# A planned four-layer graph kernel: when a PSUM bank is opened, seven-block left products in a third gated step, and ten units in the chip

## The chip, the cores and the metric

The kernel runs on one core of a Trainium2 chip. The core has a matrix engine (TensorE, written PE in the profile, with its weight loads as PEld), a vector engine (VectorE, DVE), an activation engine (ScalarE, ACT), a general engine (GpSimd, POOL) and a queue that only issues transfers (SyncE, SP). Each engine runs its own instructions in the order in which the program lists them. The metric is the device time of one execution in microseconds (us), the median of several runs. PSUM is the memory that TensorE writes its products into; the kernel treats it as eight banks of 128 partitions by 512 float32 values.

## What is computed

The input `x` is 64 graphs of 256 nodes with 128 features, all in float32, and `adj` is one 256 by 256 matrix of zeros and ones that all graphs share. Four layers follow one another, each of the form "add the layer's result to its input and normalize each node":

```
x = layernorm(x + attention_0(x, adj))            # softmax attention, plus x @ self_weight
x = layernorm(x + attention_1(x, adj))            # softmax attention, elu
x = layernorm(x + gated(x, adj))                  # five gated steps
x = layernorm(x + chebyshev(x, adj))              # products with adj, adj^2, adj^3 folded

# one gated step, of five:
m = adj @ h                                       # the "left product", per graph
z = sigmoid((m, m) @ w3.T + h @ u3.T)
r = sigmoid((m, m) @ w4.T + h @ u3.T)
v = tanh((m, m) @ w5.T + (r * h) @ u5.T)
h = (1 - z) * h + z * v
```

The gated layer is where most of the matrix work lies and where the change acts.

## The kernel before

**Tiling.** A unit is two graphs, so there are 32 units. Everything that a unit needs lies in a lane, a set of fixed tiles; `LANES = 9` lanes exist, unit `u` uses lane `u % 9`, and a lane is given to its next unit when the unit in it has issued its last instruction. So up to nine units are in the chip at once.

**The planner.** No loop sets the order of the instructions. The functions `layer0` to `layer3` only record tasks with `add(engine, ns, fn, reads, writes, after)`, where `ns` is what the planner takes the task to cost on its engine. `Plan.run` then plays the engines forward: whenever an engine is free it takes, among its tasks whose inputs are ready and for which enough PSUM banks are free, the one with the least key (`first`, line 963). The key is the unit's number times `PERIOD` plus the task's due time within its unit; due times grow along a unit's chain and are stretched by `PACE` (`PACE_GATED` in the gated layer). The last units, one for each lane, get keys that lie close together, counted back by `LATE` and `TAIL`. The instructions are emitted in the order that this gives, and each engine later executes its own in exactly that order, with waits where data is not there yet.

**PSUM banks.** A bank is taken by the first task that writes to it and is given back once every task that uses it has ended. A product whose inputs are early may therefore open a bank long before the other products that go into the same bank can run.

**The gated layer (`layer2`, line 823).** Per step and unit there is first the left product. The plain form is `left` (line 767): two graphs times two halves of the nodes, four matmuls of 128x128 by 128x256 at line 771 into one bank, and a copy of the bank to `m` by ScalarE (line 839). The fast form is `left_fast` (line 775): the two halves of the nodes and the two by two blocks of `adj` are combined so that seven matmuls of 128x128 by 128x128 (line 788) do what eight such blocks do, with three VectorE sums before them (lines 781 to 784), a ScalarE copy of one block (line 800), and four VectorE sums after them (lines 815 to 821), in two banks. Which steps use it is set by `FAST = (3, 4)`, and also asks that the step's input came by way of memory (`far`, below).

Five products by 128x512 follow, all at line 843 through the helper `product`. In the text they go by their weights: gT3, with the old state h, opens the bank `ps_g`; gT1, with m, completes the sum for r; ScalarE takes tanh of it (line 852) and VectorE forms r times h (line 854). gT2, with m, opens the bank `ps_v`; gT0, with m, is added into `ps_g` and turns the sum for r into the sum for z (line 859 takes its tanh); u5T, with r times h, completes `ps_v` (line 868 takes its tanh). VectorE then forms the new state (lines 866, 870, 872).

**Turning the state.** The next left product needs the state with nodes on the partitions. Where `far(u, step)` holds, VectorE transposes 32 by 32 blocks (lines 880, 893, 525) and transfers through a memory buffer move the blocks (`hb`, then `ht`, lines 883 to 901). Where it does not hold, TensorE does it by four transposes (line 905, and line 512 at the layer's ends), which is quicker for one unit but uses TensorE. `FIRST_FAR` makes the first two units use TensorE early on, `LAST_FAR = {0: -1, 1: 1}` makes the last unit (31) use it throughout and unit 30 from its step 1 on.

**Loading.** The first `XDIRECT = 9` units load x in its natural layout, by one transfer, and transpose it on TensorE (line 512). Later units load it by four transfers with the blocks already exchanged, and VectorE transposes the blocks (line 606).

Of the kernel before, what the change touches and what calls it, by code (L numbers as in the profile page):

```python
# [13 lines left out]
P = 128  # L14
NEG = -1.0e30
EPS = 1e-5
STEPS = 5
LANES = 9
LEAD = 10
BANKS = 8  # L20
BL = 32
FAST = (3, 4)
NORM = (0, 1, 2, 3)
SCALES = True
TIGHT = 4
FIRST_FAR = {0: 2, 1: 2}
LAST_FAR = {0: -1, 1: 1}
PERIOD = 43e3
TAIL = 0.3
LATE = 5  # L30
PACE = 2.6
PACE_GATED = 1.56
HOLD = 80
DIRECT_ROWS = 3
XDIRECT = 9
START = 35e3
R2 = 1
R3 = 1.5
# [158 lines left out]
def kernel(  # L197
# [28 lines left out]
    nc = tc.nc  # L226
# [6 lines left out]
    PE, DVE, ACT, POOL = "pe", "dve", "act", "pool"  # L233
# [12 lines left out]
    plan = Plan([psum.tile([P, 512], F32, tag=f"ps{k}", name=f"ps{k}") for k in range(BANKS)])  # L246
    add = plan.add
# [4 lines left out]
    def mm_ns(cols, n=1):  # L252
        return n * (cols * 1.667 + 5)
# [163 lines left out]
    for t, wT, n in ((wx0, woT, C0), (ws0, wselfT, D + 2)):  # L417
        ps = bank()
# [22 lines left out]
    gT = transposed("gT", [(gs[0], gs[0].ap), (gs[1], gs[1].ap), (gs[2], gs[2].ap), (u3, u3.ap)])  # L441
# [43 lines left out]
    for mc in range(NC):  # L485
        for kc in range(NC):
            add(PE, mm_ns(N), lambda mc=mc, kc=kc: nc.tensor.matmul(
                ps_a2.ap[:, mc * N : (mc + 1) * N], adj_t.ap[:, kc, mc * P : (mc + 1) * P], adjT.ap[:, kc, :],
                start=(kc == 0), stop=(kc == NC - 1)), (adj_t, adjT), (ps_a2,))
# [69 lines left out]
    def layernorm(u, L, pairs, swap=False, centred=False):  # L559

        st, ve, rstd = L["st"], L["ve"], L["rstd"]
        sts, xs = object(), object()
        for k, (c, view) in enumerate(pairs):
            add(DVE, 330, lambda k=k, view=view: nc.vector.bn_stats(st.ap[:, k, :], view().rearrange("p j d -> p d j")),  # L566
                (c,), (st,), group=sts)
        add(DVE, 150, lambda: nc.vector.tensor_scalar(  # L568
            ve.ap.rearrange("p (k j) -> p k j", k=2), st.ap.rearrange("p k (j s) -> p k j s", j=2)[:, :, :, 2], 1.0 / D, EPS,
            op0=ALU.mult, op1=ALU.add), (st,), (ve,))  # L570
        add(POOL, 1050, lambda: nc.gpsimd.tensor_tensor(rstd.ap, ve.ap, nhalf.ap, op=ALU.pow), (ve, nhalf), (rstd,))  # L571
        by_act = u >= TIGHT and plan.layer in NORM

        if by_act and not centred:
            add(DVE, 120, lambda: nc.vector.scalar_tensor_tensor(
                ve.ap.rearrange("p (k j) -> p k j", k=2), st.ap.rearrange("p k (j s) -> p k j s", j=2)[:, :, :, 1], -1.0,
                rstd.ap.rearrange("p (k j) -> p k j", k=2), op0=ALU.mult, op1=ALU.mult), (st, rstd), (ve,))
        for k, (c, view) in enumerate(pairs):
            for j in range(2):
                b, ch = (j, k) if swap else (k, j)  # L580
                at = slice(2 * k + j, 2 * k + j + 1)
                shift, col = (ones, slice(0, 1)) if centred else (ve, at)
                if by_act:
                    add(ACT, 300, lambda j=j, b=b, ch=ch, view=view, at=at, shift=shift, col=col: nc.scalar.activation(  # L584
                        X[u].ap[:, b, ch, :], view()[:, j, :], AF.Identity, bias=shift.ap[:, col], scale=rstd.ap[:, at]),
                        (c, shift, rstd), (X[u],), group=xs)
                elif centred:
                    add(DVE, 260, lambda j=j, b=b, ch=ch, view=view, at=at: nc.vector.tensor_scalar(
                        X[u].ap[:, b, ch, :], view()[:, j, :], rstd.ap[:, at], 1.0, op0=ALU.mult, op1=ALU.add),
                        (c, rstd), (X[u],), group=xs)  # L590
                else:
                    add(DVE, 260, lambda k=k, j=j, b=b, ch=ch, view=view, at=at: nc.vector.tensor_scalar(
                        X[u].ap[:, b, ch, :], view()[:, j, :], st.ap[:, k, 3 * j + 1 : 3 * j + 2], rstd.ap[:, at],
                        op0=ALU.subtract, op1=ALU.mult), (c, st, rstd), (X[u],), group=xs)
# [6 lines left out]
    def layer0(u, L):  # L601
# [7 lines left out]
        lc, d, e, p, h, u4, cu = L["m"], L["d"], L["e"], L["p"], L["h0"], L["u"], L["cu"]  # L609
        nm, s, rs = L["nm"], L["s"], L["rs"]  # L610
        hs, es, ss, ps_, ds_ = object(), object(), object(), object(), object()
        for b in range(UB):
# [5 lines left out]
            for c in range(NC):  # L618
                add(PE, mm_ns(C0), lambda b=b, c=c, hv=hv: nc.tensor.matmul(  # L619
                    hv()[:, c, :], xb[:, b, c * P : (c + 1) * P], wx0.ap, start=(c == 0), stop=True,  # L620
                    skip_group_check=True), (xT, wx0), (hx,))
# [18 lines left out]
        else:  # L640
            ds = bank()
            for b in range(UB):
                for k in range(2):
                    add(PE, 240, lambda b=b, k=k: nc.tensor.matmul(
                        ds.ap[:, b : b + 1], xb[:, b, k : N : 2], wx0.ap[:, D + 2 + k : D + 3 + k],
                        start=(k == 0), stop=(k == 1)), (xT, wx0), (ds,))
# [5 lines left out]
                neg0.ap[:, :, 0:P].rearrange("p k (c i) -> p k c i", c=NC)), (row, neg0), (e,), group=es)  # L652
        for b in range(UB):
            if SCALES and u >= TIGHT:
                add(ACT, 370, lambda b=b: nc.scalar.activation(
                    ev[:, b, :, P:N], neg0.ap[:, :, P:N], AF.Identity, bias=d.ap[:, b : b + 1]), (d, neg0), (e,), group=es)
            else:
                add(DVE, 260, lambda b=b: nc.vector.tensor_scalar_add(ev[:, b, :, P:N], neg0.ap[:, :, P:N], d.ap[:, b : b + 1]),
                    (d, neg0), (e,), group=es)
# [11 lines left out]
        tail = [add(DVE, 120, lambda: nc.vector.reciprocal(rs.ap, s.ap), (s,), (rs,))]  # L671
        hq = object()
        for g in range(G if SCALES and u >= TIGHT else 0):
            add(ACT, 270, lambda g=g: nc.scalar.activation(
                h.ap[:, g, 0 : D + 2], h.ap[:, g, 0 : D + 2], AF.Copy, scale=rs.ap[:, g : g + 1]), (h, rs), (h,), group=hq)
        if not SCALES or u < TIGHT:
            add(DVE, 700, lambda: nc.vector.tensor_mul(
# [4 lines left out]
        for b in range(UB):  # L682
            y = bank()
# [5 lines left out]
            for c in range(NC):  # L689
                add(PE, mm_ns(D + 2), lambda b=b, c=c, yv=yv: nc.tensor.matmul(  # L690
                    yv()[:, c, :], xb[:, b, c * P : (c + 1) * P], ws0.ap, start=(c == 0), stop=False,
                    skip_group_check=True), (xT, ws0), (y,), tail)
# [82 lines left out]
    def left_fast(src, blk, mat, s, p1, m):  # L775


        four = gd(s.ap)
        ss = object()

        add(DVE, 360, lambda: nc.vector.tensor_sub(
            four[:, 0:2], blk(slice(2, 3)).to_broadcast([P, 2, D]), blk(slice(0, 4, 3))), (src,), (s,), group=ss)
        add(DVE, 220, lambda: nc.vector.tensor_sub(four[:, 2:3], four[:, 1:2], blk(slice(0, 1))), (src, s), (s,), group=ss)
        add(DVE, 220, lambda: nc.vector.tensor_add(four[:, 3:4], four[:, 2:3], blk(slice(1, 2))), (src, s), (s,), group=ss)
        x, y = bank(), bank()

        def one(ps, at, lhs, k, c, cells):
            add(PE, mm_ns(P), lambda: nc.tensor.matmul(  # L788
                ps.ap[:, at * P : (at + 1) * P], lhs(), mat.ap[:, k, c * P : (c + 1) * P], start=True, stop=True,
                skip_group_check=True), (*cells, mat), (ps,), group=four)  # L790

        def a(g):
            return lambda: blk(slice(g, g + 1))[:, 0]

        def sm(k):
            return lambda: four[:, k]


        one(x, 0, a(0), 0, 0, (src,))
        add(ACT, 280, lambda: nc.scalar.copy(p1.ap[:, 0:P], x.ap[:, 0:P]), (x,), (p1,))  # L800
        one(x, 1, a(1), 1, 0, (src,))
        one(y, 3, a(3), 3, 1, (src,))
        one(y, 1, sm(0), 3, 0, (s,))
        one(y, 0, sm(1), 2, 0, (s,))
        one(x, 2, sm(2), 2, 1, (s,))
        one(y, 2, sm(3), 1, 1, (s,))
        mv = gd(m.ap)

        ms = object()

        def pv(ps):
            return gd(ps.ap)


        add(DVE, 400, lambda: nc.vector.tensor_tensor(
            mv[:, 0:4:3], pv(x)[:, 1:3], p1.ap[:, 0:P].rearrange("p (o n) -> p o n", o=1).to_broadcast([P, 2, P]), op=ALU.add),
            (x, p1), (m,))
        add(DVE, 400, lambda: nc.vector.tensor_tensor(
            mv[:, 1:3], pv(y)[:, 0:2], mv[:, 3:4].to_broadcast([P, 2, P]), op=ALU.add), (y, m), (m,))
        add(DVE, 240, lambda: nc.vector.tensor_add(mv[:, 3:4], pv(y)[:, 0:1], mv[:, 2:3]), (y, m), (m,))  # L820
        add(DVE, 400, lambda: nc.vector.tensor_add(mv[:, 1:3], pv(y)[:, 2:4], mv[:, 1:3]), (y, m), (m,))

    def layer2(u, L):
        h, ht = turned(u, L, -1), X[u]
        for step in range(STEPS):
            m = L["m"]
            fast = step in FAST and far(u, step - 1)
            ps_m = None if fast else bank()
            if fast:
# [9 lines left out]
                add(ACT, 500, lambda ps_m=ps_m: nc.scalar.copy(m.ap, ps_m.ap), (ps_m,), (m,))  # L839
            ps_g, ps_v = bank(), bank()  # L840

            def product(ps, w, c, rhs, start, stop):
                add(PE, mm_ns(T), lambda: nc.tensor.matmul(ps.ap, w(), rhs.ap, start=start, stop=stop,  # L843
                                                           skip_group_check=True), (c, rhs), (ps,))

            product(ps_g, lambda: gT.ap[:, 3], gT, h, True, False)
            product(ps_g, lambda: gT.ap[:, 1], gT, m, False, True)
            r, z, v = L["r"], L["z"], L["v"]

# [1 line left out]
            up = part if step else 1.0  # L851
            add(ACT, 600, lambda ps_g=ps_g, up=up: nc.scalar.activation(  # L852
                r.ap, ps_g.ap, AF.Tanh, bias=bias2.ap[:, 1:2], scale=0.5 / up), (ps_g, bias2), (r,))
            add(DVE, 600, lambda h=h: nc.vector.scalar_tensor_tensor(r.ap, r.ap, 1.0, h.ap, op0=ALU.add, op1=ALU.mult),  # L854
                (r, h), (r,))
            product(ps_v, lambda: gT.ap[:, 2], gT, m, True, False)
            product(ps_g, lambda: gT.ap[:, 0], gT, m, False, True)
            product(ps_v, lambda: u5T.ap[:, 0], u5T, r, False, True)
            add(ACT, 600, lambda ps_g=ps_g, up=up: nc.scalar.activation(  # L859
# [14 lines left out]
            h = new  # L874
# [128 lines left out]
```

## Time and profile before

| | before |
|---|---|
| median of 3 runs | 1424.1 us (1423.8 to 1427.39) |
| span of the profiled execution | 1422.9 us |
| TensorE busy | 1408.2 us, 99% of the span, 6009 matmul records |
| VectorE busy | 1082.7 us, 76% |
| ScalarE busy | 954.1 us, 67% |
| GpSimd busy | 141.5 us, 10% |
| transfers | 143.27 MB, 101 GB/s on average |

A float32 matmul of the program stands in the trace as two matmul records, each with a weight load of its own; a transpose is one record. Records of matmuls that run one after another overlap, [...] so the mean duration in a group (594 ns for 128x512) is longer than the distance from one start to the next. The distance is what counts for the sum of the work. It can be read off the chain that ended last, which lists unbroken runs of one kind with their length and number.

In the groups by line, the part after the bar is the busy time, the mean of one, and the idle time just before these instructions with what ended it. Idle time of VectorE and ScalarE costs nothing in itself while TensorE has other work.

### The profile page before, as it was taken

The page shows a single profiled execution, that of the slowest core. Times are in us where ns is not written, and L with a number is a line of the kernel's source. Part 1 is how long each engine was busy: PE and PEld are TensorE (multiplying, and loading weights), DVE is VectorE, ACT ScalarE, POOL GpSimd, SP SyncE. Part 2 cuts the span into 40 slices and gives each one's busy share as a digit, 9 for nine tenths or more (in the row PEclk, how much of TensorE's full clock was granted, in tenths as well). Part 3 has the DMA queues.
Part 4 walks back from the last instruction along what each step waited for, and adds up shares of the span by engine and source line. Part 5 has one row for each costly group of instructions (what it writes and reads, how often), then busy time and mean ns, then how long its engine had stood idle before and what let it go on. Part 6 is the DMA issues. An engine that isn't in the chain of part 4 may idle for free.

```text
span 1422.9 us, 19902 instructions
## 1 busy us (share of the span) xinstructions
PE 1408.2 (99%) x6009; PEld 959.7 (67%) x6009; DVE 1082.7 (76%) x2521; ACT 954.1 (67%) x2132; POOL 141.5 (10%) x134
## 2 busy tenths in 40 slices
PE   9999999999999999999999999999999999999998
PEld 8766666666766666766666666767666665666676
DVE  7977877888777787777887777878877677787642
ACT  5895564677667677667776767777866665466544
POOL 0100010101011001011101011101100000000011
PEclk9999999999999999999999999999999999999999
DMA  4223455454554554554444555544545434442222
GB/s 109 54 53 78 108 119 111 101 121 93 119 121 94 121 113 101 114 127 107 109 106 107 116 121 110 110 107 105 125 102 112 109 82 104 104 89 62 50 68 68
DMA packets 517404, 143.27 MB, mean 101 GB/s; under 512 B 445744, under 2 KB 483376, under 8 KB 517296
## 3 DMA queue, kind: packets, MB, share of 16 engines
q1 hardware_dynamic: 516496, 141.46, 44.6%
q8 instruction: 49, 0.80, 0.3%
q14 instruction: 59, 0.48, 0.1%
q10 hardware_dynamic: 800, 0.52, 0.1%
HBM read 79.26 MB, written 62.63 MB: 100 GB/s over the span
## 4 chain that ended last, share of the span: by engine, by line
PE 93%; ACT 2%; DVE 1%; DMA 1%; SPq 1%; issue 1%; POOLq 0%; ACTq 0%; DVEq 0%
PE ps L843 46%; PE ps L771 16%; PE ps L936 8%; PE ps L788 6%; PE ps L695 4%; PE ps L943 4%; PE ps L725 4%; PE ps L738 2%; PE ps L690 2%; PE ps L619 2%; DMA m<-in_x_dram 1%; ACT e L714 1%; DMA ht<-hb 1%; PE ps L905 0%; SPq L886 0%
## 5 line engine op out<-in xcount | busy, mean ns | idle before, releaser
L843 PE MATMUL ps<-m,gT 128*128 128x512 f32 x960 | 462.0, 594 | 2.4 <-ACT e L852 1.6
L571 POOL TENSOR_TENSOR rstd<-ve,nhalf 128x4 f32<-128x4 f32 x128 | 140.8, 1102 | 1276.1 <-DVE ve L568 1104.4
L843 PEld LDWEIGHTS ps<-m,gT 128*128 128x128 f32 x960 | 172.7, 190 | 138.3 <-issue 109.1
L852 ACT ACTIVATE e<-ps,bias 128x512 f32<-128x512 f32 x160 | 109.5, 686 | 107.6 <-PE ps L843 106.9
L843 PE MATMUL ps<-e,u5T 128*128 128x512 f32 x320 | 162.7, 593 | 0.0
L870 DVE SCALAR_TENSOR_TENSOR p<-e,p 128x512 f32<-128x512 f32 x160 | 109.4, 685 | 47.8 <-ACT p L868 47.0
L859 ACT ACTIVATE e<-ps,bias 128x512 f32<-128x512 f32 x160 | 110.1, 688 | 51.4 <-PE ps L843 50.3
L868 ACT ACTIVATE p<-ps,bias 128x512 f32<-128x512 f32 x160 | 109.8, 688 | 41.1 <-PE ps L843 39.4
L771 PE MATMUL ps<-adjT,x 128*128 128x256 f32 x512 | 136.2, 379 | 0.0
L839 ACT COPY m<-ps 128x512 f32<-128x512 f32 x100 | 58.2, 582 | 95.2 <-PE ps L771 94.9
L771 PEld LDWEIGHTS ps<-adjT,x 128*128 128x128 f32 x512 | 94.7, 190 | 37.2 <-issue 25.7
L771 PE MATMUL ps<-adjTp,ht 128*128 128x256 f32 x456 | 118.1, 379 | 0.4 <-DMA ht<-hb 0.4
L771 PEld LDWEIGHTS ps<-adjTp,ht 128*128 128x128 f32 x456 | 85.3, 190 | 31.3 <-issue 19.9
L843 PE MATMUL ps<-xT,gT 128*128 128x512 f32 x192 | 97.7, 593 | 0.4 <-ACT p L868 0.4
L854 DVE SCALAR_TENSOR_TENSOR e<-e,xT 128x512 f32<-128x512 f32 x96 | 65.9, 686 | 38.2 <-ACT e L852 36.0
L843 PEld LDWEIGHTS ps<-e,u5T 128*128 128x128 f32 x320 | 58.6, 190 | 47.7 <-issue 35.1
L566 DVE BATCH_NORM_STATS2 st<-ps 128x6 f32<-128x256 f32 x128 | 52.2, 424 | 42.1 <-PE ps L943 32.5
L714 ACT ACTIVATE e<-m,esd 128x256 f32<-128x256 f32 x116 | 81.0, 760 | 0.2 <-DMA m<-row 0.2
L525 DVE STREAM_TRANSPOSE p<-x 128x512 f32<-128x512 f32 x59 | 65.6, 1113 | 16.9 <-ACT x L584 10.8
L695 PEld LDWEIGHTS ps<-ht,p 128*128 128x128 f32 x512 | 65.0, 190 | 13.7 <-issue 13.2
L788 PEld LDWEIGHTS ps<-adjTf,e 128*128 128x128 f32 x480 | 62.6, 191 | 15.1 <-issue 7.8
L725 PE MATMUL ps<-p,x 128*128 128x256 f32 x256 | 69.5, 380 | 1.3 <-DVE rs L671 1.3
(174 smaller groups left out, 2576.1 us busy)
## 6 DMA issues: line engine op xcount, KB each, us to landing
hb<-p SPq DMA_DIRECT2D x176, 256.0 KB, 2.4
ht<-hb SPq DMA_DIRECT2D x468, 64.0 KB, 2.7
xT<-hb SPq DMA_DIRECT2D x236, 64.0 KB, 2.7
m<-row SPq DMA_DIRECT2D x58, 256.0 KB, 3.9
hb<-p SPq DMA_DIRECT2D x120, 64.0 KB, 1.8
ht<-hb SPq DMA_DIRECT2D x30, 256.0 KB, 2.9
out_dram<-x SPq DMA_DIRECT2D x29, 256.0 KB, 2.6
m<-in_x_dram SPq DMA_DIRECT2D x92, 64.0 KB, 2.7
```

The source lines that it names most:

```text
L571: add(POOL, 1050, lambda: nc.gpsimd.tensor_tensor(rstd.ap, ve.ap, nhalf.ap, op=ALU.pow), (ve, nhalf), (rstd,))
L695: add(PE, mm_ns(D + 2), lambda b=b, ic=ic, kc=kc, yv=yv: nc.tensor.matmul(yv()[:, ic, :], p.ap[:, b * NC + kc, ic * P : (ic + 1) * P], h.a ...
L714: add(ACT, 600, lambda g=g, b=b: nc.scalar.activation(e.ap[:, g, :].rearrange("p (c n) -> p c n", c=NC), ev()[:, b], AF.Prelu, bias=esd.ap ...
L725: add(PE, mm_ns(N), lambda b=b, jc=jc: nc.tensor.matmul(ps_x.ap[:, b * N : (b + 1) * N], X[u].ap[:, b, jc, :], p.ap[:, b * NC + jc, :], st ...
L771: add(PE, mm_ns(N), lambda b=b, mc=mc: nc.tensor.matmul(ps.ap[:, b * N : (b + 1) * N], lhs(b, mc), mat.ap[:, mc, :], start=(mc == 0), stop ...
L788: add(PE, mm_ns(P), lambda: nc.tensor.matmul(ps.ap[:, at * P : (at + 1) * P], lhs(), mat.ap[:, k, c * P : (c + 1) * P], start=True, stop=True,
L843: add(PE, mm_ns(T), lambda: nc.tensor.matmul(ps.ap, w(), rhs.ap, start=start, stop=stop, skip_group_check=True), (c, rhs), (ps,))
L852: add(ACT, 600, lambda ps_g=ps_g, up=up: nc.scalar.activation(r.ap, ps_g.ap, AF.Tanh, bias=bias2.ap[:, 1:2], scale=0.5 / up), (ps_g, bias2 ...
L859: add(ACT, 600, lambda ps_g=ps_g, up=up: nc.scalar.activation(z.ap, ps_g.ap, AF.Tanh, bias=bias2.ap[:, 0:1], scale=0.5 / up), (ps_g, bias2 ...
L868: add(ACT, 600, lambda ps_v=ps_v, up=up: nc.scalar.activation(v.ap, ps_v.ap, AF.Tanh, bias=bias2.ap[:, 2:3], scale=1 / up), (ps_v, bias2), ...
L870: add(DVE, 600, lambda: nc.vector.scalar_tensor_tensor(v.ap, z.ap, 1.0, v.ap, op0=ALU.add, op1=ALU.mult), (v, z), (v,))
L936: add(PE, mm_ns(N), lambda k=k, src=src, c=c, b=b: nc.tensor.matmul(view(c)[:, :, b, :], bn(src.ap)[:, b, c * P : (c + 1) * P], w3.ap[:, k ...
```

## The change

The change has five parts.

1. **Opening products.** gT3 of a step now also waits for the second matmul of the step's left product (`lefts[1:2]`), and gT2 for the tanh of r (`tanh_r`). Neither needs those values. The wait keeps the planner from opening the bank much earlier than the products that complete it can run. In the same spirit, the seven-block product's first matmul into its second bank waits for the last of the three VectorE sums.
2. **Seven-block left products** in steps 2, 3 and 4 instead of 3 and 4.
3. **Ten lanes** instead of nine.
4. **Turning and loading.** Unit 30 no longer turns its state on TensorE, unit 31 only from its step 1 on, and unit 8 loads x in the four-transfer form.
5. **The planner's numbers**: costs of some ScalarE tasks (lines 584, 655 and 674) and of the seven-block matmuls, `PACE` and `LATE`.

```diff
-LANES = 9
+LANES = 10
-FAST = (3, 4)
+FAST = (2, 3, 4)
-LAST_FAR = {0: -1, 1: 1}
+LAST_FAR = {0: 1}
-LATE = 5
-PACE = 2.6
+LATE = 6
+PACE = 2.9
-XDIRECT = 9
+XDIRECT = 8
...
-                    add(ACT, 300, lambda j=j, b=b, ch=ch, view=view, at=at, shift=shift, col=col: nc.scalar.activation(
+                    add(ACT, 400, lambda j=j, b=b, ch=ch, view=view, at=at, shift=shift, col=col: nc.scalar.activation(
-                add(ACT, 370, lambda b=b: nc.scalar.activation(
+                add(ACT, 420, lambda b=b: nc.scalar.activation(
-            add(ACT, 270, lambda g=g: nc.scalar.activation(
+            add(ACT, 320, lambda g=g: nc.scalar.activation(
...
-        def one(ps, at, lhs, k, c, cells):
-            add(PE, mm_ns(P), lambda: nc.tensor.matmul(
+        def one(ps, at, lhs, k, c, cells, after=()):
+            add(PE, mm_ns(P) + 4, lambda: nc.tensor.matmul(
...
-        one(y, 3, a(3), 3, 1, (src,))
+        one(y, 3, a(3), 3, 1, (src,), s.writers[-1:])
...
-            m = L["m"]
+            m, at = L["m"], len(plan.tasks)
...
-            product(ps_g, lambda: gT.ap[:, 3], gT, h, True, False)
+            lefts = [t for t in plan.tasks[at:] if t.eng == PE]
+            product(ps_g, lambda: gT.ap[:, 3], gT, h, True, False, lefts[1:2])
...
+            tanh_r = list(r.writers)
...
-            product(ps_v, lambda: gT.ap[:, 2], gT, m, True, False)
+            product(ps_v, lambda: gT.ap[:, 2], gT, m, True, False, tanh_r)
```

More of the change, by code (lines that the diff above doesn't have):

```diff
@@ L785, in left_fast @@
         x, y = bank(), bank()
-        def one(ps, at, lhs, k, c, cells):
-            add(PE, mm_ns(P), lambda: nc.tensor.matmul(
+        def one(ps, at, lhs, k, c, cells, after=()):
+            add(PE, mm_ns(P) + 4, lambda: nc.tensor.matmul(
                 ps.ap[:, at * P : (at + 1) * P], lhs(), mat.ap[:, k, c * P : (c + 1) * P], start=True, stop=True,
-                skip_group_check=True), (*cells, mat), (ps,), group=four)
+                skip_group_check=True), (*cells, mat), (ps,), after, group=four)
         def a(g):
@@ L840, in layer2, with product @@
             ps_g, ps_v = bank(), bank()
-            def product(ps, w, c, rhs, start, stop):
+            def product(ps, w, c, rhs, start, stop, after=()):
                 add(PE, mm_ns(T), lambda: nc.tensor.matmul(ps.ap, w(), rhs.ap, start=start, stop=stop,
-                                                           skip_group_check=True), (c, rhs), (ps,))
-            product(ps_g, lambda: gT.ap[:, 3], gT, h, True, False)
+                                                           skip_group_check=True), (c, rhs), (ps,), after)
+            lefts = [t for t in plan.tasks[at:] if t.eng == PE]
+            product(ps_g, lambda: gT.ap[:, 3], gT, h, True, False, lefts[1:2])
             product(ps_g, lambda: gT.ap[:, 1], gT, m, False, True)
```

## The prediction

> **What bounds the kernel now.** The page first. Part 1 says which engine is full, part 2 where it is not full, part 4 what the chain that ended last is made of.
>
> ```profile
> PE 1408.2 (99%) x6009; PEld 959.7 (67%) x6009; DVE 1082.7 (76%) x2521; ACT 954.1 (67%) x2132; POOL 141.5 (10%) x134
> PE   9999999999999999999999999999999999999998
> PEclk9999999999999999999999999999999999999999
> PE 93%; ACT 2%; DVE 1%; DMA 1%; SPq 1%; issue 1%; POOLq 0%; ACTq 0%; DVEq 0%
> ```
>
> TensorE is busy in every slice at full clock and makes up 93% of the chain. Busy time alone would not prove that it is at its rate, so I price its work. In the timeline of TensorE around 643 us, starts of neighbouring runs give the spacing of 128x128 records:
>
> ```profile
> 642.69 0.83 PE L788 MATMUL ps<-adjTf,ht 128*128 128x128 f32 x6
> 643.36 1.02 PE L843 MATMUL ps<-e,u5T 128*128 128x512 f32 x2
> 644.22 1.05 PE L788 MATMUL ps<-adjTf,e 128*128 128x128 f32 x8
> 645.11 1.46 PE L936 MATMUL ps<-w,xT 128*128 128x256 f32 x6
> ```
>
> That is 0.67/6 and 0.89/8 us: 111.5 ns for a record. The chain gives the wider ones and the transposes:
>
> ```profile
> 145.68 4.29 PE ps L843 x10
> 237.40 3.45 PE ps L771 x16
> 1368.52 0.44 PE ps L905 x4
> ```
>
> So 429 ns for 128x512, 215.6 ns for 128x256, 110 ns for a transpose. Taking every TensorE group by shape, count times spacing, all 6009 records come to 1398.0 us. The span is 1422.9 us: 24.9 us are lost. The same sum by stretch, against its length, places them: 8.2 us are lost before 60 us (filling), 0.3 between 60 and 300, 1.8 between 300 and 900, none between 900 and 1000, 5.2 between 1000 and 1210, 0.1 from there to 1400, and 6.8 after 1400 (mostly the last normalization and output, after the last matmul ends at 1416.3). The remaining 2.5 us are records counted twice at the edges of stretches. The table by stretch shows the same place as the only soft one in the middle, and VectorE's load beside it:
>
> ```profile
> core 0: us, PE busy (x) PEld busy (x) DVE busy (x) ACT busy (x) POOL busy (x), PEclk, DMA share, GB/s
> 60.00:1000.00 940.00, 939.10 (x3980) 637.21 (x3979) 745.00 (x1721) 660.40 (x1476) 97.34 (x87) 1.00 0.48 107
> 1000.00:1210.00 210.00, 207.12 (x800) 132.07 (x799) 154.27 (x332) 137.54 (x302) 16.62 (x16) 1.00 0.48 105
> ```
>
> The waits of TensorE between 900 and 1210 us name the cause: the chains of single units (tanh of r, then tanh of z and v) are late.
>
> ```profile
> PE ps L843 <- ACT e L852: 1.3, 3, 0.8
> PE ps L619 <- ACT e L859: 0.9, 1, 0.9
> PE ps L843 <- ACT p L868: 0.4, 1, 0.4
> PE ps L690 <- ACT p L868: 0.3, 1, 0.3
> ```
>
> The reading: the time is TensorE's work plus some 25 us, of which about 5 can be won in the middle.
>
> [...] records last 594 ns at a spacing of 429, hence my sum by spacing. [...] The trace does not show bank occupancy; the listed order of instructions does.
>
> **The change part by part.** I counted instructions in the two programs as they are ordered: line 771 goes from 528 matmuls to 404, line 788 from 420 to 637, line 905 from 52 transposes to 32, line 512 from 56 to 44. All other TensorE counts stay.
>
> *Seven-block products.* 217/7 = 31 more of them (units 2 to 30 gain step 2; unit 30 now also qualifies in steps 3 and 4). A plain left product is 4 matmuls, 8 records by 215.6 ns = 1.725 us; the fast one is 7 matmuls, 14 records by 111.5 = 1.561 us. 0.164 us by 31 is 5.1 us. Reading the spacings from other runs (0.67/6 to 0.89/8, 1.73/8 for 128x256) gives 4.9 to 5.4.
>
> *Transposes.* 20 + 12 fewer by 0.110 us: 3.5 us. TensorE's work is then 1398.0 - 5.1 - 3.5 = 1389.4 us.
>
> *What the fast form adds elsewhere.* On VectorE seven sums in each of 31 places: by mean durations 415 + 283 + 285 + 417 + 416 + 281 + 412 = 2.51 us, at most 78 us together. Busy time counts overlapping records once, so 2 us each is nearer: some 62 us, plus eight block transposes (0.70 or 1.11 us). VectorE goes from 1083 to about 1150 us, 82% of the new span. ScalarE loses a 582 ns copy and gains a 268 ns one each time: 10 us less. All of it lies beside TensorE, and the 60 such products of before cost it almost nothing: the page charges 0.2 us of waiting to line 821. I take zero and keep 0.2 us by 31 = 6 us for the upper end.
>
> *Transfers.* 38 more issues on 1387, with 48% of the engines' time used: zero, hidden by the units between.
>
> *Later opening.* It removes no work. The listed order, with each matmul at its spacing, says what it frees: gT3 stood ahead of gT1 by 19.3 us of TensorE work in the median and now by 6.5. The time from a bank's first product to its last matmul, summed over `ps_g` and `ps_v` in 160 steps, falls from 4800 to about 2450 us, of 8 x 1398 = 11,200. Banks no longer force the planner's hand. The added waits: gT2 is behind a tanh of 0.69 us, and everything on TensorE is behind gT2. In the new order at least 1.12 us of other TensorE work stands between gT1 and gT2 (median 2.2), gT0 among it. Lower bound zero; the upper bound, if the tanh is held up behind one long row such as the four of line 714 (2.69 us) in a tenth of the steps, is 16 x (0.69 + 2.69 - 1.12), about 36 us. I take zero, because the tenth unit and the spare banks give the order more to put there: u5T now stands at least 2.8 us behind gT1, where it stood at 1.7 us.
>
> *Ten lanes.* No work. They act in the last third, where the queue of units runs out. For each matmul I took the TensorE work between it and the last matmul that its input descends from, less the ScalarE and VectorE durations on the way. Between 900 and 1210 us the order of before has ten cases within 0.6 us, one of them negative; the new order has none from 900 to 1360. So most of the 5.2 us should close; I leave 1.0.
>
> *Head and tail.* The new order ends like the old one: eight records by 256 of line 943 behind a ScalarE copy, then one normalization. The first 60 us have the same few short distances. I keep 8.2 and 6.8 us, give or take 1.5.
>
> *Sum.* 1424.1 - 5.1 - 3.5 - 4.2 = 1411.3, so **1411 us**, 0.92% less.
>
> **The rivals.**
> *The gap stays, or moves to another place:* only the work goes, 1424.1 - 8.6 = 1415.5 us. For it: in that gap ScalarE and VectorE ran behind each other and not only their inputs, which distances do not show. Against it: the ten short distances are gone.
> *Chains of VectorE become the limit:* at 82% on average it has, by spreading its durations over the new order, stretches of 50 us above 90%. If each added seven-block product exposes the whole 1.3 us by which its four sums (spaced 0.33, 0.33, 0.21, 0.41) exceed a copy, less the 0.3 us that ScalarE saves, that is 31 us; a third of that with the gap left is 1415.5 + 10 = 1425.5 us, no change. Against it: the 0.2 us above.
> *The added waits hold up TensorE:* 16 late tanhs at 1.5 us give 1411.3 + 24 = 1435 us, slower. [...] Against it: 1.12 us or more for a tanh of 0.69.
>
> **How the numbers follow.** Chances: my forecast 0.70, with cases slightly better than it; the gap stays 0.17; VectorE limits 0.07; the waits hold up TensorE 0.06. Low end: the gap wholly gone (1.0), 5.4 for the products, 1.5 at the head, some of the 2 us of steady loss: about 1407. High end: the second case with part of the 6 us, 1418. Outside lie the last two cases and a little of the rest. Faster by over 0.3% means below 1419.8: 0.87. Within 0.3%: 0.06. Slower: 0.07.
>
> **What would show it.** Right: TensorE's records priced at these spacings come to 1389 us; lines 771 and 788 at 808 and 1274 records; the stretch before the last third's end loses under 1.5 us; no wait of line 843 on line 852 above 2 us in total; VectorE near 1150 us. Wrong: the second case if line 843 waits on line 821 for several us; the third if its waits on line 852 grow; a head longer by 3 us or more, from the ninth and tenth unit's early transfers, would be something I have not priced.

## The result and the profile after

The changed kernel takes 1408.99 us (1408.69 to 1409.65), where the kernel before took 1424.4 us in the same comparison. The ratio is 0.9888 with a 95% interval of 0.9871 to 0.9905: 1.1% faster, 2 us below the forecast of 1411 us and inside its range.

The page of the changed kernel, parts 1, 2 and 4. Lines of the program after line 843 have moved down by one to three: 852 is now 854, 868 is 871, 936 is 939, 943 is 946.

```profile
span 1406.5 us, 20482 instructions
PE 1396.0 (99%) x6163; PEld 961.8 (68%) x6163; DVE 1135.0 (81%) x2746; ACT 939.2 (67%) x2125; POOL 142.4 (10%) x134
PE   8999999999999999999999999999999999999998
PE 98%; DVE 1%; ACT 1%; DMA 0%; issue 0%; POOL 0%; SPq 0%; POOLq 0%; ACTq 0%; DVEq 0%
```

TensorE's share of the chain went from 93% to 98%: the work that ended last is now almost nothing but matmuls. VectorE has 52 us more to do in a shorter span, and after the first 30 us TensorE's waits, listed below, hardly show it. Records rose from 6009 to 6163 although the work fell, because seven narrow matmuls take the place of four wide ones. The groups of the two kinds, in the listing by shape:

```profile
L771 PE MATMUL ps<-adjT,x 128*128 128x256 f32 x512 | 135.1, 379 | 0.0
L788 PE MATMUL ps<-adjTf,e 128*128 128x128 f32 x728 | 102.9, 275 | 0.0
L788 PE MATMUL ps<-adjTf,ht 128*128 128x128 f32 x546 | 91.9, 274 | 0.0
L771 PE MATMUL ps<-adjTp,ht 128*128 128x256 f32 x240 | 64.9, 379 | 0.0
L771 PE MATMUL ps<-adjT,ht 128*128 128x256 f32 x56 | 14.4, 379 | 0.0
```

Line 771 has 808 records and line 788 has 1274, as counted. With the spacings of the prediction (429, 215.6, 111.5, 110 ns) all records come to 1389.4 us. So 17.1 us of the span are lost, against 24.9 before. The work gives 8.6 us of the shorter span and the smaller losses give 7.8. (The span of the profiled executions fell by 16.4 us, the median time by 15.4.)

Where the losses went shows in the table by stretch and in TensorE's waits. First the changed kernel, then the list of all its waits over 0.15 us in the whole run (each with its total, its number and its longest, in us).

```profile
core 0: us, PE busy (x) PEld busy (x) DVE busy (x) ACT busy (x) POOL busy (x), PEclk, DMA share, GB/s
60.00:900.00 840.00, 839.71 (x3679) 572.41 (x3678) 699.75 (x1675) 588.57 (x1335) 86.72 (x79) 1.00 0.49 108
900.00:1210.00 310.00, 310.00 (x1320) 206.57 (x1319) 256.42 (x602) 205.15 (x453) 28.95 (x24) 1.00 0.48 105
```

```profile
PE ps L725 <- DVE p L718: 2.3, 1, 2.3
PE ps L344 <- POOL ident masks.py:199: 1.4, 1, 1.4
PE ps L843 <- DVE m L821: 0.3, 1, 0.3
```

The first two waits lie in the first 30 us. After that one wait of 0.3 us is left in 1376 us. The waits of line 843 on the tanh of r are gone. Over the whole run of the kernel before they were these:

```profile
PE ps L843 <- ACT e L852: 1.6, 4, 0.8
```

Followed in the listed order, all four of them were waits of gT0, which is added into the bank that this tanh reads. They were not waits of gT2: the list given as `after` goes to the planner alone and not to the matmul, so on the chip gT2 does not wait for the tanh. It only stands later in the program.

The table below uses the prediction's measure, length of the stretch less records times spacing, for every run. Records at an edge count on both sides, so a full stretch reads about 0.4 us too low; read differences.

| run | time, us | work, us | lost before 60 | 60 to 900 | 900 to 1210 | from 1210 on |
|---|---|---|---|---|---|---|
| before | 1424.4 | 1398.0 | 8.2 | 2.5 | 5.7 | 7.3 |
| changed | 1409.0 | 1389.4 | 8.5 | 0.7 | -0.1 | 6.6 |
| changed, early opening | 1430.8 | 1389.4 | 9.3 | 8.0 | 12.3 | 7.9 |
| changed, nine lanes | 1440.1 | 1389.4 | 7.6 | 5.6 | 0.1 | 33.4 |
| changed, nine lanes, old keys | 1408.9 | 1389.4 | 8.8 | -0.3 | 0.3 | 6.7 |
| changed, gT3 late only | 1409.5 | 1389.4 | 9.8 | 0.9 | -0.3 | 6.8 |
| changed, gT2 late only | 1426.1 | 1389.4 | 8.8 | 6.3 | 10.6 | 7.5 |
| changed, seven-block in 3, 4 | 1412.4 | 1394.2 | 7.9 | -0.3 | -0.3 | 7.0 |
| changed, turning on TensorE | 1410.8 | 1393.4 | 6.5 | 0.2 | -0.5 | 6.7 |
| changed, seven banks | 1411.7 | 1389.4 | 8.8 | 3.3 | -0.4 | 6.5 |
| changed, early opening, seven banks | 1502.1 | 1389.4 | 8.2 | 28.2 | 32.1 | 35.5 |
| before, later opening | 1418.2 | 1398.0 | 7.9 | 2.1 | -0.0 | 7.1 |
| before, ten lanes | 1440.5 | 1398.0 | 6.8 | 4.6 | 17.4 | 9.8 |
| changed, seven-block in 1 to 4 | 1403.1 | 1384.5 | 6.8 | 0.0 | -0.0 | 7.1 |

### The profile page after: what moved, and what is told of

Read it like the earlier page. It is cut to its first block, busy times and chain, and to the rows that moved or that the text cites. A ratio compares the mean times of both kernels' runs of the same rounds, so it can differ in the third digit from the quotient of the medians.

```text
span 1406.5 us, 20482 instructions
## 1 busy us (share of the span) xinstructions
PE 1396.0 (99%) x6163; PEld 961.8 (68%) x6163; DVE 1135.0 (81%) x2746; ACT 939.2 (67%) x2125; POOL 142.4 (10%) x134
## 4 chain that ended last, share of the span: by engine, by line
PE 98%; DVE 1%; ACT 1%; DMA 0%; issue 0%; POOL 0%; SPq 0%; POOLq 0%; ACTq 0%; DVEq 0%
PE ps L843 48%; PE ps L771 12%; PE ps L788 10%; PE ps L939 8%; PE ps L695 4%; PE ps L725 4%; PE ps L946 4%; PE ps L690 2%; PE ps L619 2%; PE ps L738 2%; PE ps L344 0%; DMA m<-row 0%; PE ps L512 0%; PE ps L908 0%; ACT e L714 0%; PE ps L555 0%
## 5 line engine op out<-in xcount | busy, mean ns | idle before, releaser
L788 PEld LDWEIGHTS ps<-adjTf,ht 128*128 128x128 f32 x546 | 88.0, 191 | 47.6 <-issue 38.4
L788 PEld LDWEIGHTS ps<-adjTf,e 128*128 128x128 f32 x728 | 95.3, 192 | 15.0 <-issue 12.4
L788 PE MATMUL ps<-adjTf,e 128*128 128x128 f32 x728 | 102.9, 275 | 0.0
L788 PE MATMUL ps<-adjTf,ht 128*128 128x128 f32 x546 | 91.9, 274 | 0.0
L839 ACT COPY m<-ps 128x512 f32<-128x512 f32 x69 | 40.2, 583 | 70.6 <-PE ps L771 69.7
```

The costliest lines, as they stand in the source:

```text
L788: add(PE, mm_ns(P) + 4, lambda: nc.tensor.matmul(ps.ap[:, at * P : (at + 1) * P], lhs(), mat.ap[:, k, c * P : (c + 1) * P], start=True, st ...
```

## The experiments

**Opening early again.** The later opening taken back, all else kept.

```diff
-        one(y, 3, a(3), 3, 1, (src,), s.writers[-1:])
+        one(y, 3, a(3), 3, 1, (src,))
...
-            product(ps_g, lambda: gT.ap[:, 3], gT, h, True, False, lefts[1:2])
+            product(ps_g, lambda: gT.ap[:, 3], gT, h, True, False)
...
-            product(ps_v, lambda: gT.ap[:, 2], gT, m, True, False, tanh_r)
+            product(ps_v, lambda: gT.ap[:, 2], gT, m, True, False)
```

> The changed kernel, but gT3, gT2 and the first product of the seven-block form's second bank no longer wait for anything that they don't need. TensorE's work stays at 1389.4 us. Theory A (banks opened early are what crowds the planner, and the later opening closed the losses in the middle): TensorE loses 8 to 15 us again between 60 and 1385 us, most of it after 900 us, and the time is 1416 to 1424 us. Rival B (the tenth lane closed them, the opening did nothing): within 1.5 us of 1409 us.

Measured: 1430.8 us, ratio to the kernel before 1.0041 (1.0026 to 1.0056). This is slower than before, in spite of 8.6 us less work. Against the changed kernel 21.8 us are missing, more than the 8 to 15 expected, in the stretches expected and also before 900 us. TensorE's longest waits between 900 and 1300 us in this run:

```profile
PE ps L946 <- ACT e L943: 1.6, 2, 1.0
PE ps L788 <- DVE m L815: 0.9, 1, 0.9
PE ps L843 <- ACT e L854: 0.8, 1, 0.8
PE ps L771 <- ACT p L871: 0.8, 1, 0.8
PE ps L771 <- DVE m L815: 0.8, 1, 0.8
```

No one place stands out, but three of these five lines are waits for a bank. Lines 788 and 771 read neither m nor p, so the sums of line 815 and the tanh of line 871 give them no value. In the listed order each of those waits belongs to a product that opens a bank, and it ends when the last reader of the bank's previous content ends (the product at 1142.44 us starts 0.05 us after that tanh). The other two lines are waits for data. Over the whole run such bank waits come to 7.4 of the 15 us of waits that the trace lists, and the changed kernel has none. How the rest of the 21.8 us splits is not shown: pauses under 0.15 us are not listed.

**Nine lanes.**

```diff
-LANES = 10
+LANES = 9
```

> The changed kernel with nine lanes. TensorE's work stays at 1389.4 us. Theory A (later opening closed the losses): 1409 to 1411 us, under 2 us lost between 60 and 1385 us. Rival B (the tenth lane closed them): 4 to 8 us lost again after 900 us, 1413 to 1417 us.

Measured: 1440.1 us, ratio 1.0106 (1.0091 to 1.0121). Neither expectation had this. Between 900 and 1210 us nothing is lost, as theory A says; but 33 us are lost after 1210, and before 900 the loss is 5 us higher than in the changed kernel. The four longest waits from 1300 us to the end:

```profile
PE ps L771 <- ACT x L584: 6.7, 1, 6.7
PE ps L908 <- DVE p L875: 4.1, 2, 2.2
PE ps L512 <- ACT x L584: 4.0, 1, 4.0
PE ps L843 <- DVE m L821: 1.3, 1, 1.3
```

Single waits of up to 6.7 us on one unit's own chain: TensorE has run out of other units; none of this run's waits is for a bank. The granted clock also drops there: its mean is 0.95 between 1300 and 1385 us and 0.89 from 1385 us on. Behind such waits it is 0.50 for 17 us in all; TensorE is busy for 10.9 of them, so by estimate (half of 10.9) this is up to 5.5 of the 33. In this order unit 30's gated layer ends with 21 us of TensorE's work left in the list and unit 31's with 14; in the changed kernel it is 52 and 18. What brought that about, the lane or the planner's keys, is the question of a later run.

**Seven-block products in two steps.**

```diff
-FAST = (2, 3, 4)
+FAST = (3, 4)
```

> The changed kernel with seven-block products in steps 3 and 4 only: 29 units lose one each. Theory A (TensorE's work alone counts, 0.164 us for each): 4.8 us more, 1413 to 1415 us. Rival C (their VectorE sums give part of it back by late inputs): 1411 us or less, with fewer waits of line 843 than in the changed kernel.

Measured: 1412.4 us (1411.6 to 1413.0), 3.4 us more than the changed kernel. The work grew by 4.75 us as computed; the losses are 1.2 us lower in the profiled spans, 0.6 of it in the first 60 us. The time lies between the two expectations, just under theory A's 1413. Part of the discount goes with TensorE's granted clock: two of the four executions have the mean clock of 0.997 that three of the changed kernel's four have, and they took 1413.0 us, about 4.3 more than those. So theory A holds. No wait of line 843 on line 821 is left in this run, against 0.3 us in the changed kernel; rival C explains at most that much.

**Turning the last units on TensorE, and unit 8 loaded as before.**

```diff
-LAST_FAR = {0: 1}
+LAST_FAR = {0: -1, 1: 1}
-XDIRECT = 8
+XDIRECT = 9
```

> The changed kernel with the last two units turned on TensorE and unit 8 loaded as before: 32 transposes by 0.110 us come back, and unit 30 loses its three seven-block products (3 by 0.164 us). Theory A: 4.0 us more, 1412 to 1414 us. Rival D (the quicker turning shortens the chains of the last units and the end, which pays for it): 1408 to 1410 us, with less than 6 us lost after the last part of the run.

Measured: 1410.8 us (1409.9 to 1412.0), 1.9 us more, though the work grew by 4.0. Turning on TensorE is the quicker way for one unit: four transposes take 0.44 us in the chain of the changed kernel, where the two transfers of a turn through memory land after a median of 1.8 to 2.4 us (`hb`) and 2.6 to 3.2 us (`ht`). Rival D guessed a gift from this, but in the wrong place: the end costs the same (6.7 against 6.6 us), and the first 60 us lose 2.0 us less. Of the two edits only the loading of unit 8 reaches into that stretch. In the changed kernel line 725 waits 2.3 us for line 718 at 29.7 us, and in this run 1.3 us for line 671. In the changed kernel the granted clock is then 0.50 for 3.41 us (last section), which by estimate (half of 3.41) costs 1.7 us and does not happen in the profiled execution of this run. Two smaller waits of this run take 0.7 us back, which leaves the 2.0. The two executions of this run with the mean clock of 0.997 took 1411.7 and 1412.0 us, some 3 us more than the changed kernel's with the same clock. So at a like clock this part of the change brings about three quarters of what its work says. The two edits were not separated.

**The later opening alone, in the kernel before.** The waits of gT3 and gT2 as in the change, without the one in the seven-block form and with nothing else touched.

> The kernel before with only the later opening of gT3 and gT2 added: nine lanes, seven-block products in two steps, and the planner's numbers as they were. TensorE's work stays at 1398.0 us. Theory A (later opening alone closes the losses in the middle): the 9 us lost between 60 and 1400 us fall to under 3, 1416 to 1420 us. Rival E (it works only together with ten lanes and the new numbers of the planner): no gain, 1422 us or more, with new losses at the end as with nine lanes in the changed kernel.

Measured: 1418.2 us, ratio 0.9960 (0.9946 to 0.9975). The stretch from 900 to 1210 us, which lost 5.7 us, loses nothing:

```profile
60.00:900.00 840.00, 839.06 (x3530) 567.05 (x3529) 667.76 (x1529) 578.99 (x1295) 86.75 (x76) 1.00 0.48 106
900.00:1210.00 310.00, 310.00 (x1291) 208.92 (x1290) 233.59 (x533) 216.97 (x486) 29.68 (x27) 1.00 0.49 108
```

TensorE is busy for all of the 310 us, at full clock. Waits for a bank fall from 2.0 us over the run to 0.4. This part works without the others, and without more lanes. Rival E falls.

**Ten lanes alone, in the kernel before.**

```diff
-LANES = 9
+LANES = 10
```

> The kernel before with only ten lanes. Work stays at 1398.0 us. Theory A (banks are the scarce thing, and a tenth unit that opens banks early crowds them further): the losses grow after 900 us, by 4 to 12 us, 1428 to 1436 us. Rival B (a tenth unit gives TensorE more to choose from): 1418 to 1422 us.

Measured: 1440.5 us, ratio 1.0114 (1.0099 to 1.0129). A tenth unit that opens banks early costs 16 us, more than expected, and 17.4 us are lost between 900 and 1210 us. Of the 17 us of waits that the trace lists, 11.2 are for a bank. Rival B falls. The planner's numbers stayed those for nine lanes here; the early opening with ten lanes and the new numbers, above, lost 12.3 us in the same stretch.

**A bank less, with late and with early opening.** This is the test of what the later opening acts through.

```diff
-BANKS = 8
+BANKS = 7
```

> The changed kernel with seven PSUM banks instead of eight. Theory A (what later opening frees is banks, about half of their time): it does nearly as well with seven, 1409 to 1412 us. Rival F (opening matters through the order of TensorE's work, not through banks): the same small change as in the kernel that opens early and loses a bank, in which case both lose little.

> The changed kernel with the early opening of before and with seven banks. Theory A (early opening costs because it ties up banks): a bank less costs much more here than in the changed kernel, 15 us or more on top of the 1431 us that early opening takes with eight. Rival F (banks are not what is short): 1430 to 1434 us.

Measured: 1411.7 us with late opening, 2.7 more than with eight banks; 1502.1 us with early opening, 71 more. The tables by stretch, late opening first:

```profile
60.00:900.00 840.00, 837.96 (x3675) 571.56 (x3674) 698.96 (x1673) 585.39 (x1334) 85.39 (x79) 1.00 0.49 108
900.00:1210.00 310.00, 310.00 (x1317) 206.19 (x1316) 256.85 (x596) 204.82 (x449) 24.66 (x23) 1.00 0.48 105
```

```profile
60.00:900.00 840.00, 824.54 (x3570) 556.13 (x3569) 681.60 (x1632) 569.91 (x1287) 86.67 (x76) 1.00 0.47 104
900.00:1210.00 310.00, 289.89 (x1154) 183.18 (x1153) 229.56 (x520) 196.80 (x427) 26.48 (x24) 0.99 0.46 101
```

The same work, the same engines; with early opening every engine but GpSimd does less in the same time. Waits for a bank come to 1.7 us with late opening and to 43.7 with early opening. Banks are what is short, and rival F falls.

**The nine lanes again, with the planner's keys of before.**

```diff
-LANES = 10
+LANES = 9
-LATE = 6
-PACE = 2.9
+LATE = 5
+PACE = 2.6
```

> The changed kernel with nine lanes and, unlike the earlier run with nine, LATE 5 and PACE 2.6 as before. Theory G (nine lanes cost 31 us only because LATE 6 is right for ten units at the end; the tenth unit itself brings nothing): the end costs about 7 us again, 1408 to 1411 us. Rival H (the last units need the tenth lane to start early enough): still 10 us or more lost after 1300 us, 1418 us or more.

Measured: 1408.9 us (1406.8 to 1409.4), the time of the changed kernel. Losses after 1210 us are 6.7 us again. So the tenth lane is worth nothing that these runs can see, and the 31 us of the earlier run with nine lanes came from keys that do not suit nine lanes. Which of the two numbers does it was not separated.

**One wait at a time.**

```diff
-            product(ps_v, lambda: gT.ap[:, 2], gT, m, True, False, tanh_r)
+            product(ps_v, lambda: gT.ap[:, 2], gT, m, True, False)
```

> The changed kernel with the later opening of gT3 alone; gT2 opens early. gT3 stood 19 us ahead before and gT2 mostly under 4 us, so theory A says that nearly all of the 22 us of early opening come from gT3: 1409 to 1411 us. Rival I (each wait gives half): 1416 to 1424 us.

The second run takes back the other waits, on gT3 and on the seven-block form's second bank.

> The changed kernel with the later opening of gT2 alone; gT3 and the seven-block form's second bank open early. Theory A (gT3 is what ties up the banks): 1422 to 1432 us, losses over all of the middle. Rival I (each wait gives half): 1416 to 1424 us.

Measured: 1409.5 us with gT3 late alone, 1426.1 us with gT2 late alone (ratio 1.0005, 0.9998 to 1.0012). Of the 21.8 us that early opening costs, gT3's wait together with the seven-block form's saves 21.3, and gT2's by itself 4.7. The seven-block form's was not run alone. Waits for a bank come to 0.2 us with gT3 late and to 5.9 with gT2 late. The time from a bank's first product to its last matmul, summed over the 160 steps in the listed orders, says the same: 4913 us of TensorE's work with both early, 4386 with gT2 late, 3091 with gT3 late, 2452 with both.

**Seven-block products in four steps.**

```diff
-FAST = (2, 3, 4)
+FAST = (1, 2, 3, 4)
```

> The changed kernel with seven-block products in steps 1, 2, 3 and 4: 30 more, by 0.164 us, so TensorE's work falls from 1389.4 to 1384.5 us. Theory A (work alone counts as long as no waits come back): 1403 to 1405 us, under 2 us lost between 60 and 1380 us, with VectorE at 85%. Rival C (VectorE's sums, now 121 times seven, make inputs late): 1408 us or more, with waits of line 843 on line 821 of several us.

Measured: 1403.1 us (1401.9 to 1405.4), ratio to the kernel before 0.9849 (0.9834 to 0.9864). It is the fastest of all kernels here, 5.9 us below the changed one, of which 4.9 are work. The other 1.0 may be the clock: two of its four executions have a mean clock of 0.999, and none of the changed kernel's has. Its page:

```profile
PE 1389.4 (99%) x6343; PEld 961.0 (69%) x6343; DVE 1187.5 (85%) x2956; ACT 928.8 (66%) x2125; POOL 149.5 (11%) x134
PE 98%; DMA 1%; SPq 1%; ACT 0%; DVE 0%; issue 0%; POOLq 0%; POOL 0%; ACTq 0%
```

After the first 30 us VectorE at 85% still makes nothing late; no wait of line 843 is on TensorE's list.

## Why the prediction was right

*TensorE's work.* Right: 1389.4 us forecast and found. Forecast and finding share the counts and the spacings, so the agreement alone proves little; that the spacings hold is seen between 900 and 1210 us of the changed kernel, where the priced records fill 310 us to 0.1. Taken back singly, the seven-block part brings 3.4 us in time for 4.75 of work, and turning and loading 1.9 for 4.0; at a like clock 4.3 and about 3. The first figure was near; in the second I took the head as unchanged, and there the changed kernel's longer wait (2.3 us against 1.3) and its granted clock of 0.50 for 3.41 us cost it time.

*The losses.* The term was too small: I let 4.2 us of the 24.9 close, and 7.8 did. The scattered 2 us before 900 us went too (2.5 to 0.7), and of the gap after 900 nothing was left, where I kept 1.0.

*What the losses were.* The reading of TensorE's waits between 900 and 1210 us, "the chains of single units" are late, was half wrong. Of the four lines shown, only the one on line 852 is such a chain: 1.3 us of gT0 waiting for the tanh of r. The other three, 1.5 us, are waits for a bank. Lines 619 and 690 there are products of unit 28's first layer and use no tanh of the gated layer; in the listed order each of the three opens the bank that this tanh, of another unit, was the last to read. The later opening was priced through the order alone, and its direct gain on these waits was not seen.

*What closes them.* Here one step of the argument was wrong. "They act in the last third, where the queue of units runs out" gave the credit for the gap to the ten lanes, beside the spare banks. Later opening alone closes the gap in the kernel before; ten lanes alone widen it to 17.4 us; and with nine lanes and old keys the changed kernel is as fast. The distances in the listed order predicted the outcome correctly, since they were a property of the whole change, but they could not say which part made them. The step on later opening, "Banks no longer force the planner's hand", is what the seven-bank pair shows.

*The added waits.* Taken at zero; they cost nothing visible, but the step was right in part by luck. It assumed that gT2 waits for the tanh on the chip, which it does not. The product that does wait is gT0, in both kernels. The step also put gT0 between gT1 and gT2; that is so in 19 of the 160 steps. The third rival, late tanhs holding up TensorE, did not come: no wait of line 843 on the tanh is left. In the traces all 6163 TensorE records of the changed kernel and all 6009 of the kernel before stand in the listed order, so a late tanh would have held up everything behind gT0. (The 1996 activations and copies of ScalarE in the changed kernel do the same, and 2744 of VectorE's 2746 records; the other two are neighbours that start 0.02 us apart.) From the end of gT1 to gT0 the new order has at least 1.53 us of other work, where five steps of the old one had under 0.9; a tanh lasts 0.69 us in the trace.

*VectorE.* About 1150 us forecast, 1135.0 found: the added rows overlap their neighbours more than I allowed. The zero for its effect on TensorE held here, and held with 30 products more. The second rival is refuted by that run.

*Head and tail.* 8.2 and 6.8 us forecast, 8.5 and 6.6 found. That the head came out so near is chance: 1.7 us of its 8.5 are, by the estimate above, the granted clock of 0.50, and the kernel before had a granted clock of 1.00 over these 60 us.

## What to carry to other kernels

Price the busiest engine's work by spacing, stretch by stretch; the remainder shows how much reordering can win and where. A matmul that opens an accumulator early is not free because the engine had time for it: it takes a buffer that others need (early opening cost 21.8 us here with eight banks and 90 with seven), and holding it back behind a value that it does not use can be worth more than the work it delays. When one planner number is changed, its partners (here the keys of the last units with the number of lanes) have to follow, or the end can fall apart (33 us lost after 1210 us here) while most of the run looks well. And a wait can be for room and not for a value: when the waiting matmul does not read what the profile names, look for the buffer that both use.

## What the runs showed of the hardware that was not expected

The same wait can cost different times. Line 725 waits 2.26 us for line 718 near 29.6 us in the changed kernel and in the one with four seven-block steps. Here is TensorE's next run, with the clock of two stretches of 3.41 us around it, first in the changed kernel:

```profile
29.68 3.23 PE L725 MATMUL ps<-p,x 128*128 128x256 f32 x8 [2.26 <-DVE p L718]
...
26.87:30.28 3.41, 1.15 (x8) 0.86 (x7) 3.20 (x6) 3.41 (x12) 0.00 (x0) 1.00 0.01 2
30.28:33.69 3.41, 3.41 (x12) 2.88 (x11) 2.36 (x11) 2.11 (x7) 0.00 (x0) 0.50 0.07 7
```

and in the kernel with four seven-block steps:

```profile
29.55 1.99 PE L725 MATMUL ps<-p,x 128*128 128x256 f32 x8 [2.26 <-DVE p L718]
...
24.88:28.29 3.41, 2.41 (x22) 2.17 (x20) 2.57 (x12) 3.38 (x10) 0.00 (x0) 1.00 0.01 2
28.29:31.71 3.42, 2.16 (x11) 1.95 (x12) 3.27 (x13) 3.36 (x13) 0.00 (x0) 1.00 0.04 5
```

In the first the granted clock is 0.50 for 3.41 us, in the second 1.00 throughout, and eight matmuls last 3.23 or 1.99 us. In the changed kernel TensorE was busy for 1.15 of the 3.41 us before the clock of 0.50 began, at 30.28 us. There is one more such place in its trace, behind the last matmul: the clock is 0.50 from 1402.43 us to the end, and TensorE was busy for 1.07 of the 3.42 us before. The length of the wait does not decide between the two kernels, since it is 2.26 us in both; what does was not shown.

Stretches of 3.41 us at a granted clock of 0.50 cost, by an estimate from these two figures, 1.7 us of TensorE's work each, as much as some of the parts tested here. So differences of a microsecond or two between these kernels' medians are not explained by the kernels alone.
